# A graph layer with routed experts on one Trainium2 core: an early table load, statistics in the gaps of a search, and a new order of one-hots and weight parts

## The chip, the cores and the metric

One core of a Trainium2 chip runs the whole program. Its engines have in-order queues of their own: PE (TensorE, matmuls and transposes), DVE (VectorE), ACT (ScalarE), POOL (GpSimd, which here also issues the gathers) and SP (SyncE, which issues most of the other DMAs). The metric is device microseconds for one execution, lower is better.

## The reference

`x` has 2048 nodes of 256 features. There are 67,584 edges (32,768 random pairs in both directions and one loop for each node), sorted by `dst`. Cut to what matters:

```python
edge_index = jnp.stack([src, dst])
x = x + gnn(layernorm(x), edge_weight, edge_index, node_vec1)
#   gnn: out[src[e]] += edge_weight[e] * layernorm(x)[dst[e]];  plus node_vec1 on each row
x = x + ffn(layernorm(x), ...)
#   ffn: logits = x @ Wr + br, the best 2 of 8 experts for each node, weights normalised over the two,
#   each expert: layer norm with its own gain and bias, W1 (256 x 1024), exact gelu, W2 (1024 x 256)
```

## The kernel before, in words

**Two halves.** The first, up to about 222 us, is the graph layer; it also normalises `x` and computes the router's logits on the way. The second is the experts: nodes are listed by expert, their rows are gathered, and slots of 256 rows go through the two layers, PE back to back.

**The graph layer as a dense product.** The kernel turns the edge list into a dense matrix of 2048 x 2048 and multiplies. Nodes are taken in groups of two destinations (1024 groups), 128 groups to a set, so there are `GQ` = 8 sets, q = 0 to 7. Each partition of a set holds a window of 128 edges that begins at its group's first edge.

**The search.** Since `dst` is sorted, a group's first edge is found in two stages. `find_blocks` (L187) compares the first `dst` of each of 128 runs with the group's first node, `get_run(q)` (L198) gathers the run of 528 edges for each partition (POOL), and `count_before(q)` (L207) lets ACT sum `Sign(colp - run)` over it: the number of edges before the group. `get_win(q)` (L212) turns the sum into an address (`at`, `at_i` on DVE) and gathers three windows on POOL: `win_s`, `win_d`, `win_w` (source, destination, weight). ACT's table of functions for Sign is loaded ahead of the first Sign.

**Keys.** `keys_of(q)` (L245) makes two small numbers for each edge: `f[0]`, the source modulo 128, and `f[1]`, built of the source's block of 128 and the destination's place in its group (`cl` on ACT, the rest on DVE). `turn_keys(q, f)` (L258) transposes both and the weights on PE into one PSUM tile `pk`, which has a single buffer, so that edges lie on partitions; ACT copies them to bfloat16 as `k2` (the two keys) and `w2[..., 0]` (the weight). It also sums `own` on ACT, a count of the edges that the windows cover. `next_part(q, i)` (L276) splits the weight into three bfloat16 parts: DVE subtracts the part before from the rest (`r`), ACT copies `r` into `w2[..., i]`. Parts 1 and 2 each need one call.

**One-hots and columns.** There are `NH` = 32 steps n, four for each set (q = n // 4), each with 32 groups. `make_hots(n)` (L284) runs on DVE: `hl` is the one-hot of the key `k2[0]`, `eq` that of `k2[1]`, and `hr` is `eq` times the three weight parts. `make_cols(n)` (L303) multiplies them on PE (192 small matmuls into two `pa` tiles, of which there are three buffers), ACT copies each `pa` into `ar`, and SP writes `ar` to DRAM as `ad`. After each odd step SP reads the block back as `ac`, in the layout that the product needs. From step 9 on, `dense(g, b)` (L326) does the product for an earlier group of four blocks, and `add` (L335, DVE) adds its result to `acc` one step later. In the seventh of every eight steps of a group two `dense` stand in one step, in the eighth none: the double ones are at n = 15, 23 and 31, the empty ones at n = 16 and 24.

**The order is written by hand.** All of this stands in one `manual_schedule`: each engine executes its instructions in the order of the program text. Before the loop: statistics of blocks 0 to 3 (`block_stats`, L227, a `bn_stats` and a `bn_aggr` for each of 16 blocks), `count_before(0)`, `get_win(0)`, blocks 4 to 7, `count_before(1)`, `get_win(1)`, `get_run(2)`, `get_run(3)`, blocks 8 and 9, keys and transposes of set 0, keys of set 1, both further parts of set 0, the transposes of set 1, then `make_hots(0)`. In the loop, step n begins with `make_hots(n + 1)`, then:

```python
            if n % 4 == 0 and q + 1 < GQ:
                if q + 2 < GQ:
                    count_before(q + 2)
                next_part(q + 1, 1)
            elif n % 4 == 1 and q + 1 < GQ:
                if q + 2 < GQ:
                    get_win(q + 2)
                    ...
                next_part(q + 1, 2)
            elif n % 4 == 3 and q + 2 < GQ:
                f = keys_of(q + 2)
```

then the adds that are due, `make_cols(n)`, the step's `dense`, and `turn_keys(q + 2, f)` where keys were made. Step 0 ends with blocks 10 to 15 of the statistics, the square root on ACT (which loads another table) and the reciprocal `rs` on DVE. Step 1 transposes rows of parameters into a tile that takes the buffer of `pk`, copies them (`cols` on ACT) and sorts them (`by_e` on DVE). Steps 2 to 9 normalise `x`, make the logits and add `node_vec1`, on ACT and PE.

Of the kernel before, what the change touches and what calls it, by code (L numbers as in the profile page):

```python
# [9 lines left out]
F32 = mybir.dt.float32  # L10
# [3 lines left out]
AF = mybir.ActivationFunctionType  # L14
# [5 lines left out]
P = 128  # L20
# [4 lines left out]
def kernel(  # L25
# [30 lines left out]
    nc = tc.nc  # L56
# [3 lines left out]
    NB = N // P  # L60
# [5 lines left out]
    GQ = NG // P  # L66
# [27 lines left out]
    acc = consts.tile([P, NB, DX], F32, name="acc")  # L94
# [32 lines left out]
    eps_sb = consts.tile([P, 1], F32, name="eps_sb")  # L127
# [48 lines left out]
    find = pool("find", 1)  # L176
# [21 lines left out]
    def get_run(q):  # L198
        runs[q] = find.tile([P, EJ], I32, name="run", bufs=3)
        nc.gpsimd.indirect_dma_start(  # L200
            out=runs[q],
            out_offset=None,
            in_=dst.rearrange("(p j) -> p j", p=P),
            in_offset=bass.IndirectOffsetOnAxis(ap=blk_i[:, q:q + 1], axis=0),
        )

    def count_before(q):  # L207
        sign = find.tile([P, EJ], BF16, name="sign")
        nc.scalar.activation(sign, runs[q], AF.Sign, bias=colp[:, q:q + 1], scale=-1.0,
                             accum_out=at[:, q:q + 1])  # L210

    def get_win(q):  # L212
        a = at[:, q:q + 1]
        nc.vector.scalar_tensor_tensor(a, a, 0.5, mid[:, q:q + 1], op0=OP.mult, op1=OP.add)
        nc.vector.tensor_scalar(at_i[:, q:q + 1], a, float(E - P), None, op0=OP.min)
        wins[q] = []
        for name, t, dt in (("s", src, I32), ("d", dst, I32), ("w", edge_weight, F32)):
            w = find.tile([P, P], dt, name=f"win_{name}", bufs=3)
            nc.gpsimd.indirect_dma_start(  # L219
                out=w,  # L220
                out_offset=None,
                in_=one_d(t),
                in_offset=bass.IndirectOffsetOnAxis(ap=at_i[:, q:q + 1], axis=0),
            )
            wins[q].append(w)

    def block_stats(bn, mv, t, blocks):  # L227
        for b in blocks:
            nc.vector.bn_stats(bn[:, b, :], t[:, b, :D])
            nc.vector.bn_aggr(mv[:, b, :], bn[:, b, :])  # L230
# [14 lines left out]
    def keys_of(q):  # L245


        s_i, d_i, _ = wins[q]
        cl = prep.tile([P, P], F32, name="cl")
        nc.scalar.activation(cl, d_i, AF.Identity, bias=col16[:, q:q + 1], scale=float(NB))  # L250
        b_i = prep.tile([P, P], I32, name="b_i")
        nc.vector.tensor_scalar(b_i, s_i, 7, None, op0=OP.arith_shift_right)
        f = prep.tile([P, 2, P], F32, name="f")
        nc.vector.scalar_tensor_tensor(f[:, 0, :], b_i, -float(P), s_i, op0=OP.mult, op1=OP.add)  # L254
        nc.vector.tensor_tensor(f[:, 1, :], cl, b_i, OP.add)
        return f

    def turn_keys(q, f):  # L258


        pk = ps_k.tile([P, 3, P], F32, name="pk")
        for i in range(2):
            nc.tensor.transpose(pk[:, i, :], f[:, i, :], ident)  # L263
        nc.tensor.transpose(pk[:, 2, :], wins[q][2], ident)
        w2 = keys.tile([P, P, 3, 2], BF16, name="w2")
        nc.scalar.copy(w2[:, :, 0, :], pk[:, 2, :, None].to_broadcast([P, P, 2]))
        k2 = keys.tile([P, 2, P, 2], BF16, name="k2")
        for i in range(2):
            nc.scalar.copy(k2[:, i], pk[:, i, :, None].to_broadcast([P, P, 2]))
        parts[q] = (k2, w2, pk[:, 2, :])  # L270
        own = prep.tile([P, P], F32, name="own")
        nc.scalar.activation(own, wins[q][1], AF.Abs, bias=colm[:, q:q + 1], scale=1.0)
        nc.scalar.activation(own, own, AF.Relu, bias=c15, scale=-1.0,
                             accum_out=used_q[:, q:q + 1])

    def next_part(q, i):  # L276

        k2, w2, rest = parts[q]
        r = prep.tile([P, P], F32, name=f"r{i}")
        nc.vector.tensor_tensor(r, rest, w2[:, :, i - 1, 0], OP.subtract)  # L280
        nc.scalar.copy(w2[:, :, i, :], r[:, :, None].to_broadcast([P, P, 2]))
        parts[q] = (k2, w2, r)

    def make_hots(n):  # L284


        k2, w2, _ = parts[n // 4]
        g = n % 4
        hl = hotl.tile([P, GH, P], BF16, name="hl")
        nc.vector.tensor_tensor(hl.rearrange("p g (n t) -> p g n t", t=2),  # L290
                                two(k2[:, 0], g, P), pair(P), OP.is_equal)
        eq = hotr.tile([P, GH, RK], BF16, name="eq")
        nc.vector.tensor_tensor(eq.rearrange("p g (n t) -> p g n t", t=2),  # L293
                                two(k2[:, 1], g, RK), pair(RK), OP.is_equal)
        hr = hotr.tile([P, GH, 3, RK], BF16, name="hr")
        w = w2[:, g * GH:(g + 1) * GH].rearrange("p g i t -> p (g i) t")
        nc.vector.tensor_tensor(  # L297
            hr.rearrange("p g i (n t) -> p (g i) n t", t=2),
            eq[:, :, None, :].to_broadcast([P, GH, 3, RK]),
            w[:, :, None, :].to_broadcast([P, GH * 3, RK // 2, 2]), OP.mult)  # L300
        return hl, hr
# [39 lines left out]
    with tc.manual_schedule(engines=ALL):  # L341
# [9 lines left out]
        get_run(1)  # L351
        bn = small.tile([P, NB, 6], F32, name="bn", bufs=1)
        mv = small.tile([P, NB, 2], F32, name="mv", bufs=1)
        block_stats(bn, mv, acc, range(0, 4))
        count_before(0)
        get_win(0)
        block_stats(bn, mv, acc, range(4, 8))
        count_before(1)
        get_win(1)
        get_run(2)  # L360
        get_run(3)
        block_stats(bn, mv, acc, range(8, 10))
        turn_keys(0, keys_of(0))
        f1 = keys_of(1)
        next_part(0, 1)
        next_part(0, 2)
        turn_keys(1, f1)
        hots = {0: make_hots(0)}
        late = []
        NH = 2 * NB  # L370
        for n in range(NH):
            q = n // 4
            if n + 1 < NH:
                hots[n + 1] = make_hots(n + 1)
            f = None
            if n % 4 == 0 and q + 1 < GQ:
                if q + 2 < GQ:
                    count_before(q + 2)
                next_part(q + 1, 1)
            elif n % 4 == 1 and q + 1 < GQ:  # L380
                if q + 2 < GQ:
                    get_win(q + 2)
                    if q + 4 < GQ:
                        get_run(q + 4)
                next_part(q + 1, 2)
            elif n % 4 == 3 and q + 2 < GQ:
                f = keys_of(q + 2)
# [8 lines left out]
            if f is not None:  # L396
                turn_keys(q + 2, f)
            if n == 0:
                block_stats(bn, mv, acc, range(10, NB))
                sd = small.tile([P, NB], F32, name="sd", bufs=1)  # L400
                nc.scalar.activation(sd, mv[:, :, 1], AF.Sqrt, bias=eps_sb, scale=1.0)
                rs = small.tile([P, NB], F32, name="rs", bufs=1)
                nc.vector.reciprocal(rs, sd)
                shift = small.tile([P, NB], F32, name="shift", bufs=1)
                nc.vector.scalar_tensor_tensor(shift, mv[:, :, 0], -1.0, rs, op0=OP.mult,
                                               op1=OP.mult)
# [85 lines left out]
    with tc.If(n_used < E):  # L492
# [11 lines left out]
        with tc.tile_pool(name="any", bufs=2) as anyp, tc.tile_pool(  # L504
            name="ps_any", bufs=2, space=PSUM
# [606 lines left out]
```

## Time and profile before

| what | value |
|---|---|
| median of 3 runs | 516.95 us (513.53 to 521.79) |
| the profiled execution | 519.32 us, of which the span 517.6 us |
| busy in the span | PE 454.6, DVE 282.2, ACT 191.3, POOL 149.9 us |
| mean granted clock of TensorE | 0.964 |
| 0 to 54 us | DVE busy 41.00, PE 15.73, ACT 17.62 us |
| 54 to 88 us | DVE busy 30.30, PE 27.36, ACT 26.69 us |
| 88 to 211 us | PE busy 119.07, DVE 114.59 us |
| 222 us to the end | PE busy 283.48 of 295.60 us |

A row of a timeline reads: start in us, length in us, engine, line, operation, what is written and read, and in brackets how long the engine was idle before it and what ended that wait. A row of the chain reads: start, length, what. The rows of "slices" give the busy share of each fortieth of the span in tenths. DVE instructions overlap a little: the one-hot `hl` of 2.28 us is followed by the next one 2.20 us after its start.

### The profile page before, as it was taken

What the parts mean: (1) busy time and instruction counts of PE and PEld (TensorE: products, weight loads), DVE (VectorE), ACT (ScalarE), POOL (GpSimd) and SP (SyncE); (2) the same over time, 40 slices, a digit from 0 to 9 for tenths busy, and PEclk for the clock granted to TensorE, in tenths of its full rate; (3) what the DMA queues carried; (4) which work ended last, traced back from release to release, by engine and by line L of the source; (5) the groups of instructions that cost most, each with busy time, mean ns of one, the idle gap of its engine ahead of it and who ended that gap; (6) DMA issues with size and microseconds to landing.
All of it is one profiled execution on the core that took longest, in us unless ns stands there. A gap on an engine that the chain in (4) does not pass through costs nothing.

```text
span 517.6 us, 12052 instructions
## 1 busy us (share of the span) xinstructions
PE 454.6 (88%) x4996; PEld 391.2 (76%) x4996; DVE 282.2 (55%) x591; ACT 191.3 (37%) x438; POOL 149.9 (29%) x126
## 2 busy tenths in 40 slices
PE   0154787999989999899999999999999999998993
PEld 0043675888768878778888888888888888887882
DVE  5698979998999899324857333322242312212111
ACT  1524777242343222025665323232334333233320
POOL 3505032341504000000042543443553444422231
PEclk9995698999989999999999999999999999999898
DMA  6214866766575657798421898998999677226510
GB/s 209 72 42 134 235 191 229 227 186 217 157 247 178 194 164 207 220 349 296 165 63 22 258 334 264 324 357 249 298 361 316 179 212 206 40 33 202 171 65 20
DMA packets 84356, 102.15 MB, mean 197 GB/s; under 512 B 8240, under 2 KB 74656, under 8 KB 82176
## 3 DMA queue, kind: packets, MB, share of 16 engines
q1 hardware_dynamic: 74832, 86.26, 51.5%
q0 software_dynamic: 7984, 13.91, 11.6%
q10 hardware_dynamic: 1472, 1.06, 0.7%
q8 instruction: 44, 0.72, 0.5%
q14 instruction: 24, 0.20, 0.1%
HBM read 75.18 MB, written 28.14 MB: 200 GB/s over the span
## 4 chain that ended last, share of the span: by engine, by line
PE 62%; DMA 19%; DVE 9%; issue 4%; ACT 4%; POOL 1%; SPq 0%; POOLq 0%; DVEq 0%; ACTq 0%
PE py L331 19%; PE py L935 16%; PE ph L921 15%; DMA xs<-xr_d,to_i 8%; PE pa L317 6%; DVE hl L290 3%; DMA ac<-ad 2%; DMA ad<-ar 2%; DVE hr L297 2%; PE px L742 2%; DMA y_d<-ys,to_i 2%; DMA out<-y_d 2%; DMA win_w<-in_edge_weight,at_i 1%; PE py L443 1%; PE px L886 1%
## 5 line engine op out<-in xcount | busy, mean ns | idle before, releaser
L331 PE MATMUL py<-xn_sb,ac 128*128 128x264 f32 x512 | 122.9, 396 | 4.4 <-DMA ac<-ad 3.0
L921 PE MATMUL ph<-xeT,w 128*128 128x256 f32 (+1 forms) x576 | 122.7, 372 | 2.5 <-PEq L1066 1.9
L935 PE MATMUL py<-w,hT 128*128 128x256 f32 x544 | 121.0, 379 | 0.0
L921 PEld LDWEIGHTS ph<-xeT,w 128*128 128x128 f32 x576 | 105.6, 192 | 16.9 <-issue 3.3
L331 PEld LDWEIGHTS py<-xn_sb,ac 128*128 128x128 f32 x512 | 96.9, 193 | 23.8 <-DMA ac<-ad 2.8
L923 ACT ACTIVATE hT<-ph,ec 128x256 f32<-128x256 f32 (+1 forms) x144 | 66.5, 462 | 125.3 <-PE ph L921 72.9
L935 PEld LDWEIGHTS py<-w,hT 128*128 128x128 f32 x544 | 101.8, 190 | 13.0
L943 POOL DMA_INDIRECT y_d<-ys,to_i x30 | 48.6, 1620 | 118.3 <-DVE ys L938 75.5
L290 DVE TENSOR_TENSOR hl<-k,iota_b 128x4096 bf16<-128x4096 bf16 x32 | 73.1, 2285 | 3.7 <-PE pa L317 3.7
L317 PE MATMUL pa<-hl,hr 128*32 128x128 bf16 x3072 | 56.9, 236 | 19.2 <-DVE hr L297 16.8
L317 PEld LDWEIGHTS <-hr 128*32 128x32 bf16 x3072 | 50.0, 106 | 28.3 <-DVE hr L297 18.4
L895 DVE TENSOR_SCALAR xeT<-px,ec 128x256 f32<-128x256 f32 (+1 forms) x38 | 18.4, 525 | 81.6 <-PE px L886 79.7
L297 DVE TENSOR_TENSOR hr<-eq,w 128x3072 bf16<-128x3072 bf16 x32 | 56.3, 1758 | 2.0 <-DVE eq L293 0.5
L938 DVE SCALAR_TENSOR_TENSOR ys<-py,wt,b2w 128x256 f32<-128x256 f32 x34 | 16.4, 484 | 74.5 <-PE py L935 59.4
L847 POOL DMA_INDIRECT xs<-xr_d,to_i x39 | 40.4, 1037 | 55.8 <-DVE r L613 43.5
L320 ACT COPY ar<-pa 128x512 f32<-128x512 f32 x64 | 35.4, 584 | 37.6 <-PE pa L317 36.4
L219 POOL DMA_INDIRECT win_s<-in_src,at_i x8 | 11.6, 1455 | 99.0 <-DVE r L280 94.8
L336 DVE TENSOR_TENSOR acc<-acc,py 128x528 f32<-128x528 f32 x32 | 22.2, 699 | 22.6 <-PE py L331 22.4
L910 ACT ACTIVATE b2w<-b,wt 128x256 f32<-128x256 f32 x36 | 16.3, 499 | 34.4 <-DVE wt L908 28.7
L263 PE MATMUL pk<-ident,f 128*128 128x128 f32 x16 | 4.7, 348 | 20.6 <-DVE f L254 16.3
L293 DVE TENSOR_TENSOR eq<-k,iota_b 128x1024 bf16<-128x1024 bf16 x32 | 21.9, 684 | 0.0
L263 PEld LDWEIGHTS pk<-ident,f 128*128 128x128 f32 x16 | 2.4, 158 | 22.8 <-issue 13.0
(193 smaller groups left out, 308.6 us busy)
## 6 DMA issues: line engine op xcount, KB each, us to landing
w<-in_L_ffn_W SPq DMA_DIRECT2D x40, 1024.0 KB, 9.3
ad<-ar SPq DMA_DIRECT2D x32, 512.0 KB, 4.5
ac<-ad SPq DMA_DIRECT2D x16, 1024.0 KB, 5.9
b<-in_L_ffn_b SPq DMA_DIRECT2D x20, 128.0 KB, 9.9
out<-y_d SPq DMA_DIRECT2D x4, 512.0 KB, 6.4
xr_d<-rec SPq DMA_DIRECT2D x1, 1300.0 KB, 6.2
y_d<-acc SPq DMA_DIRECT2D x1, 1280.0 KB, 5.9
acc<-in_x ACTq DMA_DIRECT2D x2, 512.0 KB, 5.9
```

The source lines that it names most:

```text
L290: nc.vector.tensor_tensor(hl.rearrange("p g (n t) -> p g n t", t=2), two(k2[:, 0], g, P), pair(P), OP.is_equal)
L293: nc.vector.tensor_tensor(eq.rearrange("p g (n t) -> p g n t", t=2), two(k2[:, 1], g, RK), pair(RK), OP.is_equal)
L297: nc.vector.tensor_tensor(hr.rearrange("p g i (n t) -> p (g i) n t", t=2), eq[:, :, None, :].to_broadcast([P, GH, 3, RK]), w[:, :, None, : ...
L317: nc.tensor.matmul(pa[j * RK:(j + 1) * RK, m, :], hr[:, g, i, :], hl[:, g, :], start=(i == 0), stop=(i == 2), tile_position=(0, j * RK))
L320: nc.scalar.copy(ar[:, m0:m0 + 4, :], pa)
L331: nc.tensor.matmul(pa[:, i, :DX], acs[g * CB + c][:, b + i, :], xn_sb[:, g * CB + c, :], start=(c == 0), stop=(c == CB - 1))
L336: nc.vector.tensor_add(acc[:, b:b + 2, :], acc[:, b:b + 2, :], pa[:, :, :DX])
L847: nc.gpsimd.indirect_dma_start(out=(sets[s.set][0] if into is None else into)[:, t, :], out_offset=None, in_=(xr_d if rows is None else ro ...
L921: nc.tensor.matmul(ph, w1[:, k, c * P:(c + 1) * P], xeT[:, k, :], start=(k == 0), stop=(k == KD - 1))
L923: nc.scalar.activation(hT[:, c, :s.n * P], ph, AF.Gelu, bias=ec[:, c:c + 1], scale=1.0)
L935: nc.tensor.matmul(py, hT[:, c, t * P:(t + 1) * P], w2[:, c, :], start=(c == 0), stop=(c == KH - 1))
L943: st = nc.gpsimd.indirect_dma_start(out=y_d[:, :], out_offset=bass.IndirectOffsetOnAxis(ap=tos[s.to][:, t:t + 1], axis=0), in_=ys, in_offs ...
```

## The change

Five edits, none of which adds or removes arithmetic, but for one function value of a single column:

- An activation `sign_0` with Sign on a constant column stands ahead of the search, so that ACT's table for Sign is loaded there.
- The statistics' blocks are dealt out anew: 0 to 5, 6 to 8, 9 to 11, 12 to 14 ahead of the loop, block 15 in step 0 (before: 0 to 3, 4 to 7, 8 and 9, then 10 to 15).
- `turn_keys` copies `k2[0]` first, then the weight, then `k2[1]`.
- `make_hots(0)` is interleaved: `hl`, part 1 of set 0, `eq`, part 2 of set 0 and the keys of set 1, `hr`. The transposes of set 1 move into step 0, behind `make_cols(0)`.
- In the loop part 1 moves from steps with n % 4 = 0 to those with 1, part 2 from 1 to 2.

```diff
+    nc.scalar.activation(find.tile([P, 1], F32, name="sign_0"), eps_sb, AF.Sign)
...
-        nc.scalar.copy(w2[:, :, 0, :], pk[:, 2, :, None].to_broadcast([P, P, 2]))
         k2 = keys.tile([P, 2, P, 2], BF16, name="k2")
-        for i in range(2):
-            nc.scalar.copy(k2[:, i], pk[:, i, :, None].to_broadcast([P, P, 2]))
+        for i, t in ((0, k2[:, 0]), (2, w2[:, :, 0, :]), (1, k2[:, 1])):
+            nc.scalar.copy(t, pk[:, i, :, None].to_broadcast([P, P, 2]))
...
-    def make_hots(n):
+    def make_hots(n, between=None):
...
+        if between:
+            between[0]()
         eq = hotr.tile([P, GH, RK], BF16, name="eq")
...
+        if between:
+            between[1]()
         hr = hotr.tile([P, GH, 3, RK], BF16, name="hr")
...
-        block_stats(bn, mv, acc, range(0, 4))
+        block_stats(bn, mv, acc, range(0, 6))
         count_before(0)
         get_win(0)
-        block_stats(bn, mv, acc, range(4, 8))
+        block_stats(bn, mv, acc, range(6, 9))
         count_before(1)
         get_win(1)
         get_run(2)
         get_run(3)
-        block_stats(bn, mv, acc, range(8, 10))
+        block_stats(bn, mv, acc, range(9, 12))
         turn_keys(0, keys_of(0))
-        f1 = keys_of(1)
-        next_part(0, 1)
-        next_part(0, 2)
-        turn_keys(1, f1)
-        hots = {0: make_hots(0)}
+        block_stats(bn, mv, acc, range(12, 15))
+        f1 = []
+
+        def rest():
+            next_part(0, 2)
+            f1.append(keys_of(1))
+
+        hots = {0: make_hots(0, (lambda: next_part(0, 1), rest))}
...
                 if q + 2 < GQ:
                     count_before(q + 2)
-                next_part(q + 1, 1)
             elif n % 4 == 1 and q + 1 < GQ:
...
+                next_part(q + 1, 1)
+            elif n % 4 == 2 and q + 1 < GQ:
                 next_part(q + 1, 2)
...
             if n == 0:
-                block_stats(bn, mv, acc, range(10, NB))
+                turn_keys(1, f1.pop())
+                block_stats(bn, mv, acc, range(15, NB))
```

## The prediction

> **What bounds the kernel now.** I read the page first (slices, chain), then the chain in order of time, then DVE's waits and its timeline for the first 45 us, then PE's timeline of the dense stage.
>
> ```profile
> span 517.6 us, 12052 instructions
> ...
> PE   0154787999989999899999999999999999998993
> ...
> DVE  5698979998999899324857333322242312212111
> ...
> 12.28 0.84 ACT sign L209 x2
> ...
> 18.75 2.50 DMA win_d<-in_dst,at_i
> 21.27 0.41 ACT cl L250
> ```
>
> A slice is 12.9 us. In the first four PE is mostly idle and DVE is the busy engine; from slice 8 to the end PE is full. The chain agrees: up to about 54 us it runs through the search (ACT, POOL, window DMAs) and DVE's one-hots, later nearly always through PE. So time taken out of the first 54 us moves everything behind it, as long as the later stages keep their shape.
>
> ```profile
> DVE at L214 <- ACT sign L209: 2.3, 1, 2.3
> ...
> DVE b_i L252 <- DMA win_s<-in_src,at_i: 1.7, 1, 1.7
> DVE by_e L425 <- ACT cols L420: 1.6, 1, 1.6
> DVE f L255 <- ACT cl L250: 1.5, 2, 1.1
> ...
> DVE hr L297 <- DVE eq L293: 0.5, 1, 0.5
> DVE r L280 <- ACT w L281: 0.5, 1, 0.5
> ...
> DVE rs L403 <- ACT sd L401: 0.4, 1, 0.4
> ...
> 10.98 1.28 ACT L209 ACT_TABLE_LOAD   x1 [10.98 <-DMA run<-in_dst,blk_i]
> ...
> 26.36 1.76 DVE L297 TENSOR_TENSOR hr<-eq,w 128x3072 bf16<-128x3072 bf16 x1 [0.52 <-DVE eq L293]
> ...
> 36.89 2.28 DVE L290 TENSOR_TENSOR hl<-k,iota_b 128x4096 bf16<-128x4096 bf16 x1
> ```
>
> The columns of the waits are total us, times, longest. The reader is to see that DVE, the bound engine here, idles some 8.5 us between 11 and 44 us, in pieces of which each has a name, and that the table load stands behind the arrival of the first run, on the chain.
>
> ```profile
> 128.34 0.33 DVE L280 TENSOR_TENSOR r<-pk,w 128x128 f32<-128x128 f32 x1 [1.95 <-ACT k L269]
> ...
> 175.77 0.34 DVE L280 TENSOR_TENSOR r<-pk,w 128x128 f32<-128x128 f32 x1 [1.69 <-ACT k L269]
> ...
> 127.27 2.19 PE L317 MATMUL pa<-hl,hr 128*32 128x128 bf16 x144
> 130.67 0.85 PE L317 MATMUL pa<-hl,hr 128*32 128x128 bf16 x48 [1.20 <-ACT ar L320]
> 131.45 3.83 PE L331 MATMUL py<-xn_sb,ac 128*128 128x264 f32 x16
> ...
> 148.10 0.33 PE L264 MATMUL pk<-ident,win_w 128*128 128x128 f32 x1 [1.16 <-DMA win_w<-in_edge_weight,at_i]
> ```
>
> In the dense stage (88 to 211 us) PE runs back to back at 1.45 + 3.76 = 5.21 us a step, and DVE needs 2.20 + 0.72 + 1.68 + 0.62 = 5.22 for hl, eq, hr and one add: a tie. DVE stalls twice, at steps n = 16 and 24, because next_part(q+1, 1) comes right after PE's double dense step and reads keys that ACT has not copied yet.
>
> [...] The trace shows 1.28 us, and Sign starts 0.02 us after it: [...] so I price 1.28 alone. [...] between Sign's load and Sqrt's at 34.37 us, casts, Identity, Abs and Relu ran without another. [...] Here a window's bar is 0.94 us and it lands 2.4 to 2.5 us after its start. I count landings.
>
> **Sign's table early.** ACT's queue is free at 3.4 us (its DMA issues end at 2.35 + 1.03), so load and the one-element Sign are over by about 5, and run 0 lands at 10.9. Sign(0) starts at 10.98 instead of 12.28. DVE now has six statistics blocks (0.53 each) from 8.58 to 11.86, just as long as Sign(0)'s accumulator (11.8). So at(0) goes from 13.14 to 11.9, POOL's first window issue from 13.76 to 12.5, and all windows, issued 1.25 apart, come 1.26 earlier. Run 1 lands at 8.87 + 3.2 = 12.07, early enough: at_i(1) at about 14.4 is before POOL's turn at 16.2.
>
> **Statistics and first one-hots.** Keys(0): win_s lands at about 14.9, DVE has blocks 9 to 11 until 16.0, b_i and f follow, cl at 16.3 (win_d: 13.74 + 2.52), so f is done at 17.0. win_w lands at 17.5, pk is finished at 18.0 (before 19.26). Blocks 12 to 14 fill DVE until 18.55; ACT's first copy, now k2[0], is done at 18.4. Then in DVE's order: hl(0) 18.55 to 20.75; r(0,1) to 21.0; eq to 21.7 (it covers ACT's 0.41 copy of part 1, the 0.48 wait of before); r(0,2) to 22.0; keys(1): b_i and f to 22.4. f's second half waits for cl(1), which stands on ACT behind the copy of part 2: 22.8, a stall of 0.4. hr(0) starts at 23.05 against 26.36. That is 3.3 less, although five blocks (2.65 us) now lie ahead of it. hl(1), eq, hr(1) end at 29.3.
>
> **What is late next.** With one block left, DVE reaches the reciprocal at 29.95. Sqrt's table load now stands on ACT behind turn_keys(1), which follows make_cols(0) on PE (24.85 to 27.6, then 0.9 of transposes): three copies and own to 30.2, load to 31.5, Sqrt to 31.8. The stall grows from 0.38 to about 1.9. This is the one price of the front. hl(2) starts at 32.25 against 36.89: 4.6 less. r(1,1) now comes after hots(2), and the transposes of the parameter rows share its one PSUM buffer pk, so they wait for it: r done at 37.4, PE 1.4, ACT's cols 0.27, by_e at 39.2. A wait of 1.8 to 1.9 instead of 1.60. hl(3) at 39.55 against 44.01. r(1,2) (0.24) moves behind hots(3); keys(2) at 49.0 against 53.20. From there PE and ACT carry the chain (turn_keys(2), normalising, logits); each step is 4.2 earlier, and the dense stage, held by ad and ac of step 7, starts at 83.7 instead of 87.88. Part 2's copy now stands ahead of ar(6) on ACT and waits for hots(7): 67.5 to 67.9, ar(6) until 68.9. This lies in ACT's old idle of 1.28 before the logits' copy, and costs nothing; without that cover it would cost 1.3.
>
> **The dense stage.** At n = 16 no r waits for ACT any more; hl(18) waits only for make_cols(16), done at 128.7 in old time instead of 129.81: 1.05. PE itself gains only 0.3 there, because make_cols(17)'s second half waits for ar(16), one 0.3 us copy earlier, and the dense of step 17 for ac, issued 126.75 and landing 4.9 later at 131.65, just in time for its fourth matmul. But at(6), the gathers behind it and win_w at 148.10 follow DVE, so PE picks up the 1.0 there. At n = 24 likewise: hl(26) 1.0 earlier; PE gets 0.3 from ar, then 0.5 as make_cols(26) no longer waits for hr. Sum: 4.2 + 1.0 + 0.8 = 6.0 us. Swapped copies in turn_keys cost nothing in later sets: their keys are used steps later. In the experts' stage PE runs its 6.91 us layers back to back, weights come after the same events; I carry the 6.0 through.
>
> **The sum.** The profiled execution took 519.32 (span 517.6 and 1.7 around it): 513.3 after. It lies 2.4 above the median 516.95, which gives 516.95 - 6.0 = 511.0. The three runs spread from 513.53 to 521.79; about 2% (10.3 us) is what a measurement of this kernel can tell from no change, so I expect a gain that is real but smaller than that.
>
> **Unknown costs.** The Sqrt stall: 0.4 (if the load slips in between) to 2.6 (if ACT's ar copies come late, up to 0.7). pk's wait: 0 to +0.8. The gathers behind at(6) took 2.1 to 3.0 each on POOL and landed after 2.4 to 9.1: the 1.0 there may be 0 or 2. Together the gain is 3 to 7.5; I take 6.0.
>
> **Rivals.** (1) Only the front counts: PE and the ac transfers set the dense stage, and the two DVE stalls were covered. For it: PE's 0.3 gain and the landing at 131.65. Against it: PE did wait for win_w, which follows DVE. Gain 4.2, or 3 with the unknowns: 513.4. (2) The gain is given back: transfers shifted against each other land later, as the ac transfers do (4.7 to 8.7), or the experts' stage, where DMA is 0.91 busy, has its own pace. For it: that share. Against it: PE shows no gap there from 300 to 435. 516.5. (3) Slower: at n % 4 == 2 the copy of part 2 stands on ACT ahead of ar and waits for DVE's next one-hots, and PE has only three pa buffers. It decides when r, copy and ar (0.24 + 0.41 + 0.6) end later than PE's next half step, that is when DVE falls more than about 2.9 us behind PE. Then every one of 7 sets loses up to that wait, some 1.7: 7 x 1.7 - 6 = 6 slower, 523. Against it: before had the same order at n % 4 == 1 with waits of 0.31 only, and a dense of 3.76 lies between.
>
> **How the numbers follow.** Forecast (511.0) 0.56, rival 1 (513.4) 0.22, rival 2 (516.5) 0.13, rival 3 (523) 0.05, more than forecast (508, with shorter gathers) 0.04. The range 506 to 516.5 takes in forecast, rival 1, and half of rival 2, with 3 us for the spread of a median. Over 2% faster (below 506.6) needs spread on top of the forecast: 0.07; over 2% slower (above 527.3) only rival 3 at nearly double price: 0.04; within 2%: 0.89.
>
> **What would show it.** Right: table load at about 3.4; at(0) near 11.9; hr(0) near 23.0; a stall of about 1.9 before rs; by_e near 39.2; first full dense near 83.7; no wait of r on ACT k at n = 16 and 24; last dense some 6 earlier. Wrong: a stall at hr(0) or hl(2) of over 1 us more than given, PE waiting for ar at n % 4 == 2, or a shift that shrinks between 90 and 210 us or after 222.

## The result, and the profile after

| what | before | after |
|---|---|---|
| median of 20 runs each | 517.39 us (513.53 to 526.17) | 512.53 us (507.24 to 518.97) |
| ratio, 95% interval | | 0.9861 [0.9832, 0.9890] |
| profiled execution's span | 517.6 us | 506.9 us |

The ratio counts only runs within 1.5% of the fastest of their kernel, which leaves out 9 of the 20 after and 3 of the 20 before, so it is lower than the ratio of the medians, 0.9906. At 517.39 us it stands for 7.2 us; the medians differ by 4.9. The forecast gain of 6.0 lies between. The median of 512.53 lies within the stated range, 1.5 above the forecast of 511.0 and 0.9 below rival 1's 513.4, so the time alone does not decide between the two.

From the two pages: the TensorE clock granted in each fortieth before, then the span and the clock after.

```profile
PEclk9995698999989999999999999999999999999898
...
span 506.9 us, 12048 instructions
...
PEclk9999799999999999999999999999999999999997
```

The two profiles differ by 10.7 us, more than the ratio and the medians give. Part of that is the particular execution, as the experiments show. First the front, in ACT's and DVE's timelines.

```profile
3.42 1.28 ACT L208 ACT_TABLE_LOAD   x1 [3.42 <-issue]
...
11.95 0.16 DVE L217 SCALAR_TENSOR_TENSOR at<-at,mid 128x1 f32<-128x1 f32 x1
...
22.93 1.75 DVE L303 TENSOR_TENSOR hr<-eq,w 128x3072 bf16<-128x3072 bf16 x1
...
31.76 0.25 DVE L414 RECIPROCAL rs<-sd 128x16 f32<-128x16 f32 x1 [1.93 <-ACT sd L412]
...
39.44 0.36 DVE L436 COPY by_e<-cols 128x64 f32<-128x64 f32 x3 [2.14 <-ACT cols L431]
```

The load is over before the first run lands, DVE has no gap before `at`, and the first `hr` starts 3.43 us earlier than before. Two waits have grown: the reciprocal's (from 0.38) and that of `by_e`, the sorted parameters (from 1.60).

Then the dense stage, on DVE and PE:

```profile
122.30 2.29 DVE L292 TENSOR_TENSOR hl<-k,iota_b 128x4096 bf16<-128x4096 bf16 x1 [1.09 <-PE pa L323]
...
120.72 2.19 PE L323 MATMUL pa<-hl,hr 128*32 128x128 bf16 x144
123.82 0.85 PE L323 MATMUL pa<-hl,hr 128*32 128x128 bf16 x48 [0.90 <-ACT ar L326]
124.60 3.83 PE L337 MATMUL py<-xn_sb,ac 128*128 128x264 f32 x16
...
140.52 0.33 PE L267 MATMUL pk<-ident,win_w 128*128 128x128 f32 x1 [1.45 <-DMA win_w<-in_edge_weight,at_i]
...
185.46 0.96 PE L323 MATMUL pa<-hl,hr 128*32 128x128 bf16 x53 [1.81 <-issue]
```

At n = 16 DVE now waits for PE (1.09) and no longer for ACT's key copies (1.95). PE's wait for `ar` fell by 0.30. PE still waits for `win_w` of set 6. The last line has no counterpart in the profile of before: PE stops in the middle of a `make_cols` for 1.81 us, with nothing in the profile that it waits for. A wait like this is called a gap at issue below. (One `make_cols` is 96 products, 48 for each `pa` tile, as the counts in these lines show: 3072 over the 32 steps. The 192 given with the kernel is two steps' worth.)

### The profile page after: what moved, and what is told of

It reads as the page before. It is cut to its first block, busy times and chain, and to the rows that moved or that the text cites. A ratio compares the mean times of both kernels' runs of the same rounds, so it can differ in the third digit from the quotient of the medians.

```text
span 506.9 us, 12048 instructions
## 1 busy us (share of the span) xinstructions
PE 449.0 (89%) x4996; PEld 387.9 (77%) x4996; DVE 281.7 (56%) x591; ACT 191.0 (38%) x439; POOL 156.9 (31%) x126
## 3 DMA queue, kind: packets, MB, share of 16 engines
q0 software_dynamic: 7984, 13.91, 11.9%
## 4 chain that ended last, share of the span: by engine, by line
PE 62%; DMA 19%; DVE 7%; issue 5%; ACT 3%; POOL 1%; SPq 1%; POOLq 0%; DVEq 0%; ACTq 0%
PE py L337 18%; PE py L946 16%; PE ph L932 16%; DMA xs<-xr_d,to_i 8%; PE pa L323 6%; DMA ac<-ad 2%; DVE hr L303 2%; PE px L753 2%; DMA ad<-ar 2%; DMA y_d<-ys,to_i 2%; DMA out<-y_d 1%; DMA win_w<-in_edge_weight,at_i 1%; DVE hl L292 1%; PE px L897 1%; PE py L454 1%
## 5 line engine op out<-in xcount | busy, mean ns | idle before, releaser
L337 PE MATMUL py<-xn_sb,ac 128*128 128x264 f32 x512 | 120.5, 391 | 4.4 <-DMA ac<-ad 3.0
L932 PE MATMUL ph<-xeT,w 128*128 128x256 f32 (+1 forms) x576 | 121.0, 368 | 2.1 <-PEq L1077 1.5
L932 PEld LDWEIGHTS ph<-xeT,w 128*128 128x128 f32 x576 | 104.5, 190 | 15.9 <-issue 2.9
L337 PEld LDWEIGHTS py<-xn_sb,ac 128*128 128x128 f32 x512 | 95.2, 190 | 23.2 <-DMA ac<-ad 3.2
L323 PE MATMUL pa<-hl,hr 128*32 128x128 bf16 x3072 | 57.0, 239 | 13.6 <-DVE hr L303 10.7
L222 POOL DMA_INDIRECT win_s<-in_src,at_i x8 | 11.6, 1450 | 83.5 <-DVE r L282 80.6
L283 ACT CAST w<-r 128x256 bf16<-128x256 f32 x16 | 6.7, 417 | 49.2 <-DVE r L282 49.2
L222 POOL DMA_INDIRECT win_w<-in_edge_weight,at_i x8 | 18.7, 2336 | 2.4 <-issue 2.4
```

Source lines behind the costliest of these rows:

```text
L222: nc.gpsimd.indirect_dma_start(out=w, out_offset=None, in_=one_d(t), in_offset=bass.IndirectOffsetOnAxis(ap=at_i[:, q:q + 1], axis=0),)
L323: nc.tensor.matmul(pa[j * RK:(j + 1) * RK, m, :], hr[:, g, i, :], hl[:, g, :], start=(i == 0), stop=(i == 2), tile_position=(0, j * RK))
L337: nc.tensor.matmul(pa[:, i, :DX], acs[g * CB + c][:, b + i, :], xn_sb[:, g * CB + c, :], start=(c == 0), stop=(c == CB - 1))
L932: nc.tensor.matmul(ph, w1[:, k, c * P:(c + 1) * P], xeT[:, k, :], start=(k == 0), stop=(k == KD - 1))
```

## The experiments

Theory A: the gain is the sum of shifts that the trace of before gives, 4 to 5 us at the front and 1.8 in the dense stage; what the two profiles differ beyond that is PE's speed in the particular execution. Rivals: B, the new order itself keeps PE's clock up; the prediction's rival 1, that PE and the `ac` transfers set the dense stage; and that the early load was covered anyway. Chips differ in level: the kernel before has a median of 526.83 us on the chip of `after_again`, `no_sign`, `old_parts` and `sqrt_first`, and of 517.4 and 517.2 on those of the other runs. So whole times and ratios are compared within a chip. Distances between two events of one profile are also set side by side across chips, which is weaker.

Three events recur. "Keys of set 2" is the start of DVE's `b_i` for that set. "The transposes of n" are those of the weights' window `win_w` at the end of step n, for n = 3, 7 and so on. "The first full dense" is where the first `dense` goes on after its wait for `ac`: six of its products run earlier.

### The changed kernel again, twice, and the kernel before again

No edit. First `after_again`:

> The changed kernel once more, unaltered, for a second profile. Theory A (the gain is the sum of own shifts, 4 to 5 us at the front and 1.8 in the dense stage; the other 3 to 4 us between the two profiles are TensorE's clock, which differs by execution): the same order of events up to the keys of set 2 at 49.3 +- 0.3 us, but low-clock stretches in other places, span 507 to 515, ratio 0.985 to 0.992. Rival B (the new order itself keeps the clock up between 37 and 60 us): granted clock again 0.95 to 1.00 from 32 to 50 us and at most one short low stretch up to 75 us, first 10 matmuls of the dense stage at 82.5 to 83.5, span 506 to 509. Also open: the 1.8 us gap on PE at 183.65 put down to issue; by A it is gone or elsewhere.

Its front kept step: first `hr` 22.30, reciprocal's wait 1.93, `by_e` 2.14, keys of set 2 at 48.66 (0.6 earlier than in the first profile, a little more than expected). But between 39 and 65 us the granted clock was 0.63 (0.94 and 0.80 in the two halves of that stretch in the first profile of after), and the first full dense started at 89.18 instead of 82.82: 40.5 us behind the keys of set 2 instead of 33.5. The order that B said would hold the clock did not. At that clock its span, 519.9 us, is no measure of the change; the ratio was 0.9855 [0.9816, 0.9894], the medians 519.53 and 526.83. The gap at issue came back, at the same matmul of the same step.

On another chip, `after_third` and `before_again`:

> The changed kernel unaltered, beside v4 and v4_warm on the same chip, for a third profile. Theory A with the clock by execution: front events as before (first hr 22.3 to 23.0, reciprocal stall 1.93, by_e wait 2.14, keys of set 2 at 48.7 to 49.3), ratio 0.984 to 0.990, and the first full dense anywhere from 82.8 to 89 us, by PE's clock between the keys of set 2 and there.

> The kernel before, unaltered, for a second profile. Theory A: same waits of DVE at the front (2.3 for the sign, 1.7 for win_s, 1.6 for cols, 1.1 for cl) and of r at n = 16 and 24, keys of set 2 at 52.6 to 53.3, with low-clock stretches in other places than in the first profile.

The ratio of `after_third` was 0.9874 [0.9844, 0.9905], the median 510.96 against 517.20. `before_again` had the waits of before (2.39, 1.84 and 1.60 us for sign, `win_s` and `cols`). `after_third` missed its expectations in part: the reciprocal's wait was 1.60, not 1.93, behind transposes of set 1 that took 0.57 us on PE (0.90 in the first profile), the keys of set 2 came 0.2 early, and the first full dense started at 80.64, before the stated 82.8, though the clock from 39 to 65 us was 0.71, below the first profile's 0.87. So the clock of that stretch alone does not set this start. The two profiles, spans 506.0 and 513.7, have the same mean granted clock (0.972) and are called the fair pair here:

| event, us | before_again | after_third | earlier by |
|---|---|---|---|
| first `hr` | 25.90 | 22.43 | 3.47 |
| `hl` of step 2 | 36.43 | 31.31 | 5.12 |
| keys of set 2 | 52.75 | 48.46 | 4.29 |
| first full dense | 86.35 | 80.64 | 5.71 |
| `win_w` transposed at n = 11 | 99.96 | 95.23 | 4.73 |
| the same at n = 15 | 124.75 | 119.96 | 4.79 |
| the same at n = 19 | 145.95 | 140.42 | 5.53 |
| the same at n = 23 | 171.08 | 165.21 | 5.87 |
| double dense of n = 31 | 207.83 | 202.02 | 5.81 |
| first dense of the last group | 216.62 | 210.81 | 5.81 |
| end of span | 513.7 | 506.0 | 7.7 |

Even this pair is not equal everywhere: right behind the wait for `ac` the ten products took 3.83 us in `after_third` and 2.49 in `before_again`, which is why the shift falls from 5.71 to 4.73. Up to the last group of the dense product the shift is 5.8 us; the last 1.9 come after it, in instructions that both kernels share. From that event to the end the two profiles of before take 298.2 and 297.1 us, the first and third of after 296.0 and 295.2, `no_sign` below 298.9, `sign_only` 296.0. So the tail varies by more than these 1.9 without following the change, and why it varies stays open.

### Without the early Sign, and with it alone

```diff
 no_sign, against the changed kernel
-    nc.scalar.activation(find.tile([P, 1], F32, name="sign_0"), eps_sb, AF.Sign)
 sign_only, against the kernel before
+    nc.scalar.activation(find.tile([P, 1], F32, name="sign_0"), eps_sb, AF.Sign)
```

> The changed kernel without the early Sign, all else as changed. Theory A (the table load is 1.28 us on the path of the windows): table load at about 11.0, at(0) at 13.2 instead of 11.95, first hr at 24.2 instead of 22.93, keys of set 2 at 50.5 instead of 49.3; 1.25 us slower than the changed kernel throughout, ratio to before about 0.989. Rival (the load was covered by statistics and the windows' landing): first hr within 0.4 of 22.93.

> The kernel before with the early Sign alone. Theory A: at(0) at 11.9 instead of 13.14, first hr at 25.1 instead of 26.36, the reciprocal at 35.3 instead of 36.51, keys of set 2 at 52.0 instead of 53.2; ratio to before about 0.9975. Rival (statistics of before fill the gap anyway): first hr within 0.4 of 26.36.

ACT's timeline of `no_sign` has the load back behind the run's arrival:

```profile
10.73 1.28 ACT L212 ACT_TABLE_LOAD   x1 [10.73 <-DMA run<-in_dst,blk_i]
12.02 0.73 ACT L212 ACTIVATE sign<-run,colp 128x528 bf16<-128x528 int32 x1
```

`at` came at 12.88 with a wait of 1.79 before it, the first `hr` at 23.94 and the keys of set 2 at 50.30, which is 1.64 later than in `after_again` and 1.44 later than in `old_parts`, both on the same chip. The load's 1.28 us lay on the path; the rest is mostly when the run landed. The ratio 0.9878 [0.9793, 0.9964] cannot tell 1.3 us.

`sign_only` (another chip) hit its expectation to 0.05 us: `at` 11.93, first `hr` 25.10, reciprocal 35.26, keys of set 2 at 51.95. That close a hit is in part luck, since run 0 landed within 0.1 us of its time in the first profile of before, and 0.4 us earlier in `before_again`. Its ratio, 0.9987 [0.9963, 1.0012], is compatible with 0.9975 and with nothing.

The landing can be taken out. From it to `at` are 2.16, 2.16 and 2.15 us in the two profiles of before and in `no_sign`, and 0.86 in `sign_only` and all three of after. So the early Sign is worth 1.30 us, and the rival of a covered load is wrong. From `at` to the first `hr` are 13.22, 13.15 and 13.17 us in the old order (`sign_only` is the last) and 10.98, 10.89, 10.94 and 11.06 in the new (`no_sign` is the last). So about 2.2 us, the larger part of the gain at the first `hr`, belong to the new order of statistics, copies and one-hots. No run takes those three edits apart.

### The weight parts back at their old steps

```diff
                     count_before(q + 2)
+                if q >= 1:
+                    next_part(q + 1, 1)
...
-                next_part(q + 1, 1)
-            elif n % 4 == 2 and q + 1 < GQ:
+                next_part(q + 1, 1 if q == 0 else 2)
+            elif n % 4 == 2 and q == 0:
                 next_part(q + 1, 2)
```

> The changed kernel with the weight parts of sets 2 to 7 put back to steps with n % 4 = 0 and 1; set 1 and the front as changed. Theory A: front unchanged (first hr 22.9, keys of set 2 at 49.3), DVE waits again for ACT's key copies at n = 16 and 24 by 1.7 to 2.0 each, and the dense stage, from its first full start to the step after n = 26, is 1.8 us longer (1.0 seen at win_w of set 6, 0.8 at n = 24 to 26). Rival 1 of the prediction (PE and the ac transfers set this stage): DVE's waits come back but PE's events from the dense start to n = 27 keep their distances within 0.5 us.

DVE's timeline of this kernel has the two waits again, at n = 16 and 24:

```profile
128.26 0.34 DVE L282 TENSOR_TENSOR r<-pk,w 128x128 f32<-128x128 f32 x1 [1.90 <-ACT k L271]
...
175.34 0.33 DVE L282 TENSOR_TENSOR r<-pk,w 128x128 f32<-128x128 f32 x1 [2.35 <-ACT k L271]
```

The second is longer than the 1.7 to 2.0 expected. PE's distance from the transposes of n = 15 to those of n = 19 was 21.31 us (21.03 and 21.20 in the profiles of before, on other chips); with the parts moved it was 20.00, 20.56, 20.46 and 20.46 in the three of after and `no_sign`.

The whole stretch, from the transposes of n = 15 to the double dense of n = 31, is best compared with `no_sign`, on the same chip and alike from the dense stage on but for the parts. Here are the transposes of n = 23 and that double dense in `old_parts`, the same two in `no_sign`, and the gaps at issue behind n = 23 in `after_third` (two) and `before_again`:

```profile
174.07 0.27 PE L267 MATMUL pk<-ident,win_w 128*128 128x128 f32 x1
210.09 7.39 PE L337 MATMUL py<-xn_sb,ac 128*128 128x264 f32 x32
...
174.57 0.27 PE L267 MATMUL pk<-ident,win_w 128*128 128x128 f32 x1
209.65 7.39 PE L337 MATMUL py<-xn_sb,ac 128*128 128x264 f32 x32
...
184.84 0.95 PE L323 MATMUL pa<-hl,hr 128*32 128x128 bf16 x53 [1.30 <-issue]
196.36 0.52 PE L323 MATMUL pa<-hl,hr 128*32 128x128 bf16 x23 [0.32 <-issue]
...
202.18 0.52 PE L317 MATMUL pa<-hl,hr 128*32 128x128 bf16 x23 [0.83 <-issue]
```

From n = 15 to n = 31 `old_parts` takes 83.10 us and `no_sign` 81.33, each with one gap at issue of 0.42: a difference of 1.77, where theory A gave 1.8. Of it 0.85 lie before n = 19 and 0.94 behind n = 23, so both stalls are worth what was forecast for them, and rival 1 is wrong.

The changed kernel itself shows less of it. Its stretch is 81.6 and 82.1 us in the first and third profile (85.6 in `after_again`, at a lower clock), against 83.5 and 83.1 before. From n = 23 to n = 31, `after_third` takes 36.81 and `before_again` 36.75: without their gaps at issue (1.62 and 0.83) they would differ by 0.73, with them nothing is left of the second stall's gain. The time of the whole kernel, 0.9895 [0.9791, 0.9998], is too uncertain to add to this.

### The square root ahead of the key copies

```diff
             if n == 0:
-                turn_keys(1, f1.pop())
                 block_stats(bn, mv, acc, range(15, NB))
                 ...
                 nc.scalar.activation(sd, mv[:, :, 1], AF.Sqrt, bias=eps_sb, scale=1.0)
+                turn_keys(1, f1.pop())
```

> The changed kernel with block 15 and the square root ahead of turn_keys(1) in step 0, so that the table load is on ACT before the key copies. Theory A (the 1.93 us stall before rs is the load standing behind the copies, and DVE sets the pace up to the keys of set 2): stall 0.3 to 0.6, keys of set 2 at 47.7 to 48.0, 1.4 us earlier than the changed kernel, carried to the end. Rival C (the start of the dense stage is set by ACT and PE steps that do not follow): stall gone, but the ad of step 7 no earlier than 72.0.

```profile
29.68 0.25 DVE L414 RECIPROCAL rs<-sd 128x16 f32<-128x16 f32 x1 [0.38 <-ACT sd L411]
```

The stall is 0.38 again, the keys of set 2 come at 47.21 (48.66 in `after_again`, 48.86 in `old_parts`), 1.45 earlier. The first full dense moved by 1.2 us (87.97 against 89.18) with similar clocks, 0.58 and 0.63 between 52 and 65 us. The sign given for rival C, a time for the `ad` of step 7, means nothing at clocks this low; beside `after_again` the start did follow, which speaks against C. That the 1.4 us are carried to the end is not shown: by the transposes of n = 11 the two profiles are level (104.30 and 104.21), with 0.88 us of gaps at issue in `sqrt_first` just before. Ratio 0.9837 [0.9779, 0.9896] beside 0.9855.

### Two waits of DVE less, and then an earlier fetch

`v2` is `sqrt_first` with the copies `by_e` and the product `wc` moved to step 2; `v3` adds the search one step earlier from set 3 on; `v4` is `v2` with the windows of set 2 and run 4 fetched in step 0 instead of step 1. Each diff shows only what is new.

```diff
 v2, beside sqrt_first
+            if n == 2:
                 by_e = consts.tile([P, NE, KH + 2 * KD], F32, name="by_e")
 v3, beside v2: get_win and get_run in n % 4 == 0 where q >= 1, and
                 f = keys_of(q + 2)
+                if q + 3 < GQ:
+                    count_before(q + 3)
 v4, beside v2, and the same calls gone from n == 1
                     count_before(q + 2)
+                if n == 0:
+                    get_win(2)
+                    get_run(4)
```

> As sqrt_first (square root ahead of turn_keys(1)), and the copies by_e and the product wc on DVE moved from step 1 to step 2, behind its one-hots. Theory A (DVE sets the pace to the keys of set 2; its waits of 1.93 and 2.14 us are on the path): keys of set 2 at 45.2 instead of 48.7 to 49.3 us, no wait of by_e, 3.5 us less in all, ratio to before about 0.979. Rival C (behind the keys of set 2 the path is ACT's normalising and PE's logits, which DVE's gain does not move): keys at 45.2, but first ad of step 7 and dense start no earlier than with sqrt_first.

> As v2, and from set 3 on the search one step earlier: count_before in steps with n % 4 = 3, the windows' gathers in those with 0. Theory A (PE's wait of 1.2 to 2.3 us for win_w of set 6 is the gathers' length behind at(6)): that wait is gone, and PE from the transposes of n = 15 to those of n = 19 takes 18.5 to 19.2 us instead of 20.0 to 20.6; 1 to 2 us less than v2. Rival: the earlier gathers delay ad and ac transfers, which set PE's start of step 17, and the sum does not change.

`v2` had its keys of set 2 at 45.63 us, 3.7 before those of after, and yet its first full dense at 82.74, where after had 82.82, and a ratio of 0.9864 [0.9823, 0.9905], short of the 0.979 expected. The gain was gone within 4 us, as PE's timeline shows:

```profile
46.23 0.69 PE L266 MATMUL pk<-ident,f 128*128 128x128 f32 x2 [3.11 <-DVE f L257]
49.60 0.48 PE L267 MATMUL pk<-ident,win_w 128*128 128x128 f32 x1 [2.68 <-DMA win_w<-in_edge_weight,at_i]
```

The keys were early and the weights' window was not: its gather was issued third, at 41.59 us, and landed at 49.6. Neither theory A nor rival C had said so. `v3` removed PE's wait for `win_w` of set 6 (18.2 us from n = 15 to n = 19 instead of 20.1), but from n = 15 to n = 23 it took 44.85 us and `v2` 44.96: PE waited instead, mainly for DVE's add (1.03 at 162.15). Behind n = 23 it also waited 0.56 for `ac`, as the rival of that expectation would have it. The ratio was 0.9884 [0.9844, 0.9925], no gain over `v2`. That an earlier window only moves the wait in this stage fits the prediction's count, 5.22 us a step for DVE and 5.21 for PE. Then `v4`, on another chip:

> As v2, with the search's windows of set 2 and run 4 fetched in step 0 instead of step 1 (5.5 to 6 us earlier). Theory D (v2's 3.6 us at the keys of set 2 were lost at once to a wait of PE for win_w of set 2, whose three gathers were issued only at 35.9 us and landed at 49.6): no wait of PE for win_w there, its transposes done by 47.0 instead of 50.0, dense start 2.5 to 3 us earlier than v2 at the same clock, ratio 0.978 to 0.983. Rival C (ACT's normalising and PE's logits hold the dense start): transposes at 47.0, dense start within 0.7 of v2's 82.7.

PE waited no longer for `win_w` of set 2, the transposes ended at 46.3, and the first full dense started at 78.97: 3.8 us before `v2`'s (on another chip, and at a clock of 0.73 from 39 to 65 us where `v4` had 0.86) and 1.7 before `after_third`'s. Its keys of set 2 were 3.4 before those of `after_third`; 1.3 of that went into a longer wait for `ac`, 3.26 us instead of 1.95. Ratio 0.9817 [0.9767, 0.9866], median 508.06 beside 510.96 for `after_third` and 517.20 for before on this chip. That is the lowest ratio of the study without extra work, but its interval overlaps those of after and of `v2`: the earlier transposes are shown, a gain of the whole kernel over `v2` is not.

### PE kept busy with filler

```diff
+        fill = ps_s.tile([P, 2, 512], F32, name="py1")
+        def keep_busy(k):
+            for i in range(k):
+                nc.tensor.matmul(fill[:, 0, :P], ones, ones, start=True, stop=True)
+        keep_busy(30)
...
         turn_keys(0, keys_of(0))
+        keep_busy(16)
...
             make_cols(n, *hots.pop(n))
+            keep_busy({1: 20, 2: 6, 3: 6}.get(n, 0))
```

> The changed kernel with 78 extra 128 x 128 float32 matmuls of a constant into an unused PSUM tile, placed where PE waits for DVE: 30 before the keys of set 0, 16 behind their transposes, 20, 6 and 6 behind make_cols of steps 1 to 3. Theory W (the low-clock stretch that every profile shows somewhere between 26 and 90 us comes from PE being idle in pieces before, and its length, which differs by execution, makes most of the spread): granted clock 0.95 or more from 26 to 78 us, the stage from the keys of set 2 to the first full dense takes 33.5 us as in the fastest profile (49.3 to 82.8) or up to 1 less, ratio to before 0.975 to 0.982. Rival (the clock differs by execution whatever PE does): a low stretch of 10 us or more again between 26 and 90, ratio 0.985 to 0.99. Fillers that run late would show as a first hr or make_cols delayed by over 0.5 us.

The first `make_cols`, in PE's timelines of after and of `warm`, and what after's granted clock was around it (columns: stretch, its length, busy us of PE, PEld, DVE, ACT, POOL, then PEclk, DMA share, GB/s):

```profile
24.74 2.75 PE L323 MATMUL pa<-hl,hr 128*32 128x128 bf16 x96 [6.59 <-DVE hr L303]
...
24.70 1.52 PE L323 MATMUL pa<-hl,hr 128*32 128x128 bf16 x96 [1.55 <-DVE hr L303]
...
24.00:30.00 6.00, 4.25 (x127) 3.65 (x131) 5.76 (x6) 3.61 (x10) 1.50 (x1) 1.00 0.37 120
```

The same 96 products take 2.75 or 1.52 us, a factor of 1.8, at a recorded clock of 1.00 either way: 2.75 in after, where PE had stood idle for 6.59 us before them, and 1.52 in `warm`, where 5.4 us of filler ended 1.55 us before them. What sets which of the two it is was not shown: step 1's group took 1.52 in `after_third` without any filler, behind 1.34 us of idle time. Because `make_cols` of step 0 and the transposes behind it were faster, Sqrt's stall was 0.43 and the wait of `by_e` 1.59, and the keys of set 2 came at 47.20. From there to the first full dense it took 33.0 us (33.5 in the first profile of after). The ratio was 0.9808 [0.9761, 0.9854], as theory W had it. But the low-clock stretch, which W was to remove, did not go away: 0.87 from 39 to 65 us, the same as in the first profile of after.

> As v4, with 74 filler matmuls at the places of warm (30, 16, 16, 6, 6). Theory W: make_cols of steps 0 to 3 take 1.5 us each instead of 2.75, the stage behind the keys of set 2 runs with fewer stretched matmuls, the times of single executions lie closer together than 6 us, ratio 0.970 to 0.976. Rival: fillers bring nothing beyond what v4 has, because their gain in warm lay in the Sqrt and by_e waits that v4 does not have: ratio as v4 within 0.003.

`v4_warm`, on the chip of `v4`, had 0.9822 [0.9781, 0.9862] and a median of 508.53 beside 508.06 of `v4`. That meets the rival of the expectation, by which filler gains only by shortening waits that `v4` does not have, though intervals this wide would also hide 2 us. Theory W failed: the executions spread over 10 us (506.18 to 516.19), and in the profiled one, 516.19 us, the products of step 0 took 1.52 us but those of step 1 2.75 in spite of the filler.

## Why the prediction was right

**The front, step by step.** In the first profile: load at 3.42 (3.4 forecast), `at` 11.95 (11.9), first `hr` 22.93 (23.05), the reciprocal's stall 1.93 (about 1.9), `hl` of step 2 at 32.14 (32.25). Counting landings and DVE's order gave these to 0.15 us. The other two profiles of after have the first `hr` 0.5 to 0.6 earlier, since the run landed earlier, so part of this closeness is luck; the distances are not. Two terms were taken alone and held: the Sign (1.26 forecast, 1.30 measured) and the price of the Sqrt load (1.5 forecast, 1.45 at the keys of set 2 by `sqrt_first`). The rest of the front, 2.2 us, came as forecast in sum only. One term was mis-sized: the wait of `by_e` was 2.14, not 1.8 to 1.9, because PE's transposes of the parameter rows took 1.7 us (37.40 to 39.12), not 1.4. Behind filler, in `warm`, they took 1.1.

**From there to the dense stage.** The forecast carried 4.2 us. The keys of set 2 were 3.90 early in the first pair and 4.29 in the fair pair, but the first full dense, forecast at 83.7, was at 82.82 and 80.64, 5.06 and 5.71 early. At the transposes of n = 15 the shift was 6.55 and 4.79. The change from one to the other lies in the ten products behind the wait for `ac`: 3.98 us before and 2.49 after in the first pair, 2.49 and 3.83 in the fair pair. So this term was too small, by 0.6 to 1.5 us, with the speed of PE in the particular execution in it. That the stage follows the keys is shown only as long as the window is there: `v2` moved the keys 3.7 further and gained nothing that shows.

**The dense stage.** Here the mechanism was right, and so was its size: both stalls of `r` are gone, the first is worth 0.85 (1.0 forecast) and came through `win_w` as argued, the second 0.94 (0.8 forecast), both by `old_parts` beside `no_sign`. In the changed kernel itself the fair pair shows 0.74 for the first and nothing for the second, because PE lost about as much at issue in the same steps, which no term of the forecast had. Moving parts onto n % 4 = 2 cost nothing on PE in these profiles: no wait for `ar` at those steps, as rival 3 would have had it.

**The sum.** 6.0 forecast; 5.8 in the fair pair up to the last group. There the front gave 4.8 (4.2 forecast), the dense stage 1.8 without the gaps at issue (1.8 forecast), and the gaps took back 0.8 (not forecast). That two of these errors, 0.6 and 0.8, cancelled is luck. By whole times the gain is 7.2 us by the first ratio, 6.5 by the fair pair's (0.0126 x 517.2), and 4.9, 7.3 and 6.2 by the medians of the three comparisons. So 6.0 is within what the measurements allow, and they do not settle it to better than about 1 us. The 2% that the prediction named as the least a measurement can tell was too coarse: the interval [0.9832, 0.9890] tells 1.4% from no change. Rival 2, that the experts' stage gives the gain back, is wrong: the tail was no longer in any profile of after than before.

## What to carry to other kernels

A wait that goes uncovers the next one, and it can be named before the edit: list, for the instruction that moves forward, every operand with its landing time. `v2` had two of three operands early and gained nothing that shows; one fetch moved by a step in `v4` brought the third operand forward by 3.6 us. Where two engines tie, removing one's wait pays only as far as the other has room: `v3` took PE's wait for `win_w` of set 6 away, and from n = 15 to n = 23 it needed 44.85 us where `v2` needed 44.96. And to size a change of 1%, compare distances between events, on one chip, and look at where the clock was low: an equal mean clock is not enough (0.972 in both of the fair pair, yet the same ten products took 3.83 and 2.49 us), and spans of single executions of one kernel here differed by more than the change is worth (506.0 to 519.9 us in the three profiles of after).

## What the runs showed of the hardware that was not expected

- One group of 96 small matmuls took 2.75 or 1.52 us behind idle time (6.59 and 1.55 us, in `after` and `warm`), with 1.00 in the granted clock both times, and the two changed by execution at the same place: step 1's took 2.75 in the first profile of after and 1.52 in `after_third`.
- PE stopped for 1.3 to 1.9 us behind the 43rd product of one `make_cols` in `after`, `after_again`, `after_third`, `v2`, `v3` and `v4`, and in no other kernel, `no_sign` included, which differs from `after` by one activation. In `after` the 16 DMA engines were over 0.9 busy when it began, at 183.65 us, and until 185.1; at the same step of `before`, from 192.9 to 194.6 us, they were over 0.9 busy too, and PE ran on, its 96 products in 1.73 us. So this traffic alone does not make the gap. What PE waited for was not tried and stays open.
